# A fused attention and feed-forward stack on one core: half of q's transposes moved, a product in one instruction, the PE stream aligned in the last layer, and the output step split off

## The chip, the core and the metric

The kernel runs on one core of one Trainium2 chip, as one launch. The metric is the device time of a run in microseconds (us). Engines: PE (TensorE, matmuls and transposes; PEld is its weight load), DVE (VectorE), ACT (ScalarE), POOL (GpSimd), and SP, whose queue issues nearly all DMAs. PSUM is the accumulator memory that PE writes and DVE and ACT read; POOL works in SBUF.

## The reference, cut to what matters

Inputs are `x` of 8 x 512 x 128 in float32 and the weights. Two blocks follow one another, each as `x = x + layernorm(block(layernorm(x)))`:

```python
x = x + _layernorm(attn(_layernorm(x)))       # Taylor-expanded attention, 16 heads
y = _layernorm(x)
for i in range(6):                            # DEPTH
    y = attn_layer(shift_tokens(y), Wqkv[i], ...) + y      # local attention, window 32
    y = ffn_layer(shift_tokens(y), ...) + y                # layer norm, 128 -> 2x341, gelu, 341 -> 128
x = x + _layernorm(y)
```

`attn_layer` projects to q, k and v (16 heads of 64), scales q and k to unit length, multiplies by rotary tables (`q*cos + rotate_half(q)*sin`, with scales), takes scores over the block's own and the previous 32 keys, a softmax, and a product with v and `Wo`.

## The kernel before, in words

The first block takes the first 532 us and is not touched. After that the work is cut into **units**: one unit is 128 tokens (`j`, 4 per sequence) of one sequence (`b`, 8) in one layer (`l`, 6), 192 in all. Four units in a row make a **group** (one sequence in one layer). The stream between layers is kept transposed, features on partitions, in `state[b]`.

One pass of the main loop, number t, runs different stages of several units. `at(t, lag, step)` calls a step for unit t - lag; with `ends=True` only where that unit is the last of its group. The order of these calls is PE's order (`manual_schedule(engines={PE})`); a scheduler in the build orders the other engines, by priority (program order; `high_priority` goes first) and its own estimate of when operands are ready. PE's order in one pass before the change:

1. `proj` (lag 0, twice: q, then k): 8 matmuls into a PSUM tile `mm`. DVE multiplies the tile by the tables: `turned(0)`, `turned(1)` (L447, halves exchanged), `straight` (L454). ACT squares it (L462, `sq`); POOL adds the products (L470).
2. `by_keys` (lag 2): 8 transposes of the softmax weights `pe` in two `tr` tiles, copied by ACT to `pT` (L588).
3. `out_project` (lag 3): 16 matmuls into `py` of tag `s`; DVE adds `py` to `state` in two halves (L632).
4. `by_features(0)` (lag 1): 4 transposes of q and 4 of k, a `tr` tile each, copied by ACT to `qT` and `kT` (L536).
5. `weigh_values` (lag 2): 128 small matmuls `po` (L598), tag `s`; DVE multiplies by the softmax's inverse sums (L606, `on`).
6. `by_features(4, 0)`: the other 4 transposes of q, one `tr` tile.
7. `values` (lag 0): 4 matmuls into `mm`, copied later by ACT (L502, in `spread`, which also issues the DMAs that make `v2`).
8. `by_features(4, 1)`: the other 4 transposes of k.
9. By group: `feed_norm` (t%4 = 2), `feed_first` (t%4 = 3), `feed_middle` (t%4 = 0: 12 matmuls with gelu on ACT), `feed_last` (t%4 = 1: 6 matmuls, then DVE adds to `state`, L696).
10. `scores` (lag 1): mask matmuls (L551) and 128 small matmuls `sp` (L558), tag `s`; then a maximum on DVE (L566) and 16 exponentials on ACT (L570).
11. `out_by_features` (lag 2): 8 transposes of `on` in two `tr` tiles, copied by ACT to `oT` (L620).

PSUM tags: `tr` has two buffers of one bank, `mm` two of two banks, `s` **one** of two banks. So a `tr` tile waits until ACT has copied the tile two before it, and `po` waits until the two additions of `py` to `state` are done.

In the last layer `feed_last` also makes the result, in the same step: DVE writes `fs` (L696), PE transposes it (4 transposes, a `tr` tile), DVE takes statistics of that tile in PSUM (L115, L117), ACT makes the inverse root (L104, L106), DVE scales out of PSUM (L127, `fo`), POOL adds `xr` (L707), SP sends it out.

ACT changes its function table twice a group: `gelu_only` (L91) before the gelus, tied behind ACT's last copy to `pT`, and `log_and_exp` (L85) behind the last gelu.

PE's instruction stream is padded at two places: `addr_align(FILL)`, FILL = 16, in `feed_hidden`, and once a group at t%4 = 1 `addr_align(128, offset=IN_STEP)`, which puts the next instruction at place 98 of 128. The condition `t <= len(units) - NB * (B - 1)` is t <= 164, so the last such place is t = 161; passes from 165 on have none.

Of the kernel before, what the change touches and what calls it, by code (L numbers as in the profile page):

```python
# [8 lines left out]
F32 = mybir.dt.float32  # L9
BF16 = mybir.dt.bfloat16  # L10
AF = mybir.ActivationFunctionType
ALU = mybir.AluOpType
# [3 lines left out]
P = 128  # L16
DM = 128
H = 16
# [3 lines left out]
NEG = -(2.0**100)  # L22
EPS = 1e-5
FILL = 16
IN_STEP = 98


@with_exitstack
def sandwich_kernel(ctx: ExitStack, tc: tile.TileContext, ins: dict, out: bass.AP):
    nc = tc.nc  # L30
    x_d = ins["L0_attn_hidden_states"]
    B, N, _ = x_d.shape
    NB = N // P
    assert B >= 2
    DEPTH = ins["L0_ffn_Wqkv"].shape[0]
# [42 lines left out]
    def transposed(ps, src, rows, cols):  # L78
        nc.tensor.transpose(ps[:cols, :rows], src, ident[:rows, :rows])  # L79


    tables, exps, divisions, copies, pcopies, maxima = [], [], [], [], [], []

    def log_and_exp(behind):
        ld = nc.scalar.preload_act_table_set("natural_log_exp_and_others")  # L85
# [3 lines left out]

    def gelu_only():  # L90
        ld = nc.scalar.preload_act_table_set("gelu_and_others")  # L91
        issue_behind(ld, pcopies[-1])
        tables.append(ld)

    def issue_behind(later, earlier):
        tc.add_manual_dep(
            later.ins, earlier.ins.name,
            mybir.DependencyInfo(mybir.DependencyClass.NoSync, mybir.DependencyReason.DATA),
            reason="order on an engine",
        )  # L100
# [7 lines left out]
    def layer_norm(pool, dst, src, nb, by_log=False, later=False):  # L108


        st = pool.tile([P, nb, 6], F32, tag="ln_st", name="ln_st")
        mv = pool.tile([P, nb, 2], F32, tag="ln_mv", name="ln_mv")
        rs = pool.tile([P, nb], F32, tag="ln_rs", name="ln_rs")
        for j in range(nb):
            nc.vector.bn_stats(st[:, j, :], src[:, j, :])  # L115
        for j in range(nb):
            nc.vector.bn_aggr(mv[:, j, :], st[:, j, :])  # L117
        if by_log:
            inverse_root(rs, mv[:, :, 1], eps)
        else:  # L120
            nc.vector.tensor_scalar(rs, mv[:, :, 1], EPS, None, ALU.add)
            nc.scalar.activation(rs, rs, AF.Sqrt)
            nc.vector.reciprocal(rs, rs)

        def last(behind=None):
            for j in range(nb):
                t = nc.vector.tensor_scalar(  # L127
                    dst[:, j, :], src[:, j, :], mv[:, j, 0:1], rs[:, j : j + 1], ALU.subtract, ALU.mult
                )
                if behind is not None:  # L130
                    issue_behind(t, behind)

        if later:
            return last
        last()
# [8 lines left out]
    HF = HD // 2  # L144
# [282 lines left out]
    def proj(u, s):  # L427

        L, b, j = u["L"], u["b"], u["j"]
        wqkv, tab = L["wqkv"], L["tab"]  # L430
        lhs = state[b][:, j * P : (j + 1) * P]
        if s == 0:
            u["ss"] = f2.tile([P, 2, H], F32, tag="ss", name="ss")
            u["qk"] = f2.tile([P, 2, H, 2, HF], F32, tag="qk", name="qk")
        ss, qk = u["ss"], u["qk"]

        ps = psum.tile([P, 2, H, HF], F32, tag="mm", name="mm")
        for a in range(2):
            nc.tensor.matmul(  # L439
                ps[:, a].rearrange("p h d -> p (h d)"), lhs, wqkv[:, s, a, :], start=True, stop=True  # L440
            )
        sq = f2.tile([P, H, 2, HF], F32, tag="sq", name="sq")
        t1 = f2.tile([P, 2, H, HF], F32, tag="t1", name="t1")
        t2 = f2.tile([P, 2, H, HF], F32, tag="t2", name="t2")

        def turned(a):
            nc.vector.tensor_tensor(  # L447
                t2[:, a], ps[:, 1 - a],
                tab[:, 2 * s + 1, j, HF * a : HF * (a + 1)].unsqueeze(1).to_broadcast([P, H, HF]),
                ALU.mult,  # L450
            )

        def straight():
            nc.vector.tensor_tensor(  # L454
                t1, ps,
                tab[:, 2 * s, j, :].rearrange("p (a d) -> p a d", a=2).unsqueeze(2)
                .to_broadcast([P, 2, H, HF]),
                ALU.mult,
            )

        def squared(a):
            nc.scalar.activation(sq[:, :, a, :], ps[:, a], AF.Square)  # L462

        turned(0)
        turned(1)
        straight()
        squared(0)
        squared(1)
        u["sq", s] = sq
        nc.gpsimd.tensor_tensor(qk[:, s].rearrange("p h a d -> p a h d"), t1, t2, ALU.add)  # L470
# [109 lines left out]
    def by_keys(u):  # L580
        pe = u["pe"]
        u["pT"] = pT = f1.tile([P, NP, P], F32, tag="pT", name="pT")
        for c in range(0, NP, 4):
            ps = psum.tile([P, 4, P], F32, tag="tr", name="tr")
            for i in range(4):
                transposed(ps[:, i, :], pe[:, c + i].rearrange("p a k -> p (a k)"), P, P)
            with tc.high_priority():
                pcopies.append(nc.scalar.copy(pT[:, c : c + 4, :], ps))  # L588

    def weigh_values(u):  # L590

# [91 lines left out]
    def feed_last(u):  # L683
        L, l, b, gT = u["L"], u["l"], u["b"], u["gT"]
        py = psum.tile([P, N], F32, tag="mm", name="py")
        for c, (c0, cn) in enumerate(CH):
            nc.tensor.matmul(  # L687
                py, L["w2"][:cn, c, :], gT[:cn, c, :], start=(c == 0), stop=(c == NCH - 1)
            )
        last = l == DEPTH - 1  # L690
        if last:
            fs = f1.tile([P, N], F32, tag="xnT", name="fs")
        for a in range(2):
            r = slice(HD * a, HD * (a + 1))
            sl = state[b][r, a : N + a]
            nc.vector.scalar_tensor_tensor(  # L696
                fs[r] if last else sl, py[r], b2_c[r, l : l + 1], sl, ALU.add, ALU.add
            )
        if last:
            ps = psum.tile([P, NB, P], F32, tag="tr", name="tr")  # L700
            for j in range(NB):
                transposed(ps[:, j, :], fs[:, j * P : (j + 1) * P], P, P)
            fo = f1.tile([P, NB, DM], F32, tag="xn", name="fo")
            layer_norm(f2, fo, ps, NB, by_log=True)
            xr = f1.tile([P, NB, DM], F32, tag="xr", name="xr")
            nc.sync.dma_start(xr, x1[b])
            nc.gpsimd.tensor_tensor(fo, fo, xr, ALU.add)  # L707
            nc.sync.dma_start(out[b].rearrange("(n p) d -> p n d", p=P), fo)

    log_and_exp(None)  # L710
    units = []
# [6 lines left out]
    def at(t, lag, step, *args, ends=False):  # L718
        if 0 <= t - lag < len(units) and (not ends or units[t - lag]["j"] == NB - 1):
            step(units[t - lag], *args)  # L720
# [3 lines left out]
    with tc.manual_schedule(engines={mybir.EngineType.PE}):  # L724
        norm_in(0)
        in_by_features(0)
        project_qk(0)
        project_v(0)
        sums_before(0)
        layers[0] = load_layer(0)  # L730
        for k in range(len(steps) + 2):
            slot(k)
        for t in range(len(units) + 7):
            if t < len(units):
                u = units[t]
                if u["l"] not in layers:
                    layers[u["l"]] = load_layer(u["l"])
                u["L"] = layers[u["l"]]


            gelus = 0 <= t - 5 < len(units) and units[t - 5]["j"] == NB - 1
            at(t, 0, proj, 0)
            at(t, 0, proj, 1)


            if t % NB == 1 and NB < t <= len(units) - NB * (B - 1):
                nc.tensor.addr_align(128, offset=IN_STEP)
            at(t, 2, by_keys)
            if gelus:
                gelu_only()  # L750
            at(t, 3, out_project)

            if t == 0:
                head_norm(NG - 1)
            if t == 1:
                attn_out(B - 1)
            at(t, 1, by_features, 0)
            at(t, 2, weigh_values)
            at(t, 1, by_features, 4, 0)
            at(t, 0, values)  # L760
            if t == 3:
                to_state(B - 1)
            at(t, 0, sum_squares, 0)
            at(t, 0, sum_squares, 1)
            if not gelus:
                at(t, 0, unit_length)
            at(t, 1, by_features, 4, 1)
            at(t, 0, spread)
            at(t, 3, feed_norm, ends=True)
            at(t, 4, feed_first, ends=True)  # L770
            at(t, 5, feed_middle, ends=True)
            if gelus:
                at(t, 0, unit_length)
            at(t, 6, feed_last, ends=True)
            at(t, 1, scores)
            at(t, 3, feed_normed, ends=True)
            at(t, 2, out_by_features)

# [90 lines left out]
```

## Time and profile before

| | us |
|---|---|
| median of 3 runs | 3826.05 (3818.64 to 3838.03) |
| the profiled execution | 3825.62 |
| its span, first to last instruction | 3823.9 |
| first block, up to the first `proj` | 532.3 |
| a group of four units in layers 1 to 4 | 66.5 to 67.0 |
| groups from unit 168 on (last layer) | 69.9, 75.1, 70.0, 74.8, 70.0 |
| from the start of unit 191 to the end | 86.4 |

The profile is of one execution. Its timeline gives the start and length of instructions, merged where neighbours are alike; a difference of two starts is the time that a piece holds the engine. Lengths of PE pieces run over into the next piece, because matmuls are pipelined. The chain of waits names as releaser the instruction that the profile infers; where that had long been done, it was another.

### The profile page before, as it was taken

The page shows a single profiled execution, that of the slowest core. Times are in us where ns is not written, and L with a number is a line of the kernel's source. Part 1 is how long each engine was busy: PE and PEld are TensorE (multiplying, and loading weights), DVE is VectorE, ACT ScalarE, POOL GpSimd, SP SyncE. Part 2 cuts the span into 40 slices and gives each one's busy share as a digit, 9 for nine tenths or more (in the row PEclk, how much of TensorE's full clock was granted, in tenths as well). Part 3 has the DMA queues.
Part 4 walks back from the last instruction along what each step waited for, and adds up shares of the span by engine and source line. Part 5 has one row for each costly group of instructions (what it writes and reads, how often), then busy time and mean ns, then how long its engine had stood idle before and what let it go on. Part 6 is the DMA issues. An engine that isn't in the chain of part 4 may idle for free.

```text
span 3823.9 us, 152697 instructions
## 1 busy us (share of the span) xinstructions
PE 3703.6 (97%) x65600; PEld 2456.2 (64%) x65600; DVE 2794.7 (73%) x4308; ACT 2662.9 (70%) x6750; POOL 1842.6 (48%) x1311
## 2 busy tenths in 40 slices
PE   8999999999999999999999999999999999989997
PEld 4545556666666666666666666666666666666664
DVE  4555567787877778787777778777777878777774
ACT  5565557777777777777777777777777777767665
POOL 0000025555555555555555655555555555555552
PEclk9999999999999999999999999999999999999998
DMA  2000012222232222322222322223222222222221
GB/s 82 17 9 12 6 51 72 60 67 62 73 79 69 66 58 66 81 73 62 67 66 58 88 72 67 57 67 82 71 65 65 67 58 65 65 67 69 64 67 32
DMA packets 153219, 233.66 MB, mean 61 GB/s; under 512 B 32622, under 2 KB 53356, under 8 KB 151788
## 3 DMA queue, kind: packets, MB, share of 16 engines
q1 hardware_dynamic: 152556, 223.89, 22.8%
q8 instruction: 530, 8.68, 0.9%
q14 instruction: 133, 1.09, 0.1%
HBM read 24.54 MB, written 4.19 MB: 8 GB/s over the span
## 4 chain that ended last, share of the span: by engine, by line
PE 95%; issue 2%; ACT 2%; DVE 1%; POOL 0%; DMA 0%; POOLq 0%; SPq 0%; DVEq 0%; ACTq 0%
PE tr L79 20%; PE mm L439 17%; PE py L627 9%; PE mm L497 9%; PE po L598 8%; PE sp L558 8%; PE y L300 4%; PE mm L652 3%; PE mm L654 3%; PE py L687 3%; PE sc L270 3%; PE sp L551 2%; PE vv L248 2%; PE qk L239 1%; PE po L336 1%
## 5 line engine op out<-in xcount | busy, mean ns | idle before, releaser
L470 POOL TENSOR_TENSOR qk<-t,t 128x1024 f32<-128x1024 f32 x384 | 909.9, 2370 | 679.3 <-DVE t L454 405.3
L486 POOL TENSOR_TENSOR qk<-qk,ss 128x1024 f32<-128x1024 f32 x384 | 722.2, 1902 | 16.0
L439 PE MATMUL mm<-wqkv,state 128*128 128x512 f32 x1536 | 698.4, 597 | 2.6 <-ACT v L502 2.6
L447 DVE TENSOR_TENSOR t<-mm,tab 128x512 f32<-128x512 f32 x768 | 498.6, 671 | 239.5 <-PE mm L439 239.5
L570 ACT ACTIVATE pe<-sp,mx 128x64 f32<-128x64 f32 x3072 | 652.1, 381 | 2.3 <-DVE mx L566 2.3
L462 ACT ACTIVATE sq<-mm 128x512 f32<-128x512 f32 x768 | 421.3, 607 | 118.6 <-DVE t L454 114.0
L454 DVE TENSOR_TENSOR t<-mm,tab 128x1024 f32<-128x1024 f32 x384 | 468.4, 1220 | 5.9
L439 PEld LDWEIGHTS mm<-wqkv,state 128*128 128x128 f32 x1536 | 273.7, 191 | 289.6 <-issue 242.2
L473 DVE TENSOR_REDUCE ss<-sq 128x16 f32<-128x1024 f32 x384 | 448.6, 1209 | 0.7 <-ACT sq L462 0.6
L79 PE MATMUL tr<-ident,qk 128*128 128x128 f32 x3072 | 440.7, 276 | 1.8 <-ACT qT L536 0.8
L536 ACT COPY kT<-tr 128x512 f32<-128x512 f32 x384 | 225.6, 587 | 299.6 <-PE tr L79 299.4
L79 PEld LDWEIGHTS tr<-ident,qk 128*128 128x128 f32 x3072 | 351.0, 141 | 120.7 <-issue 100.8
L627 PE MATMUL py<-oT,wo 128*128 128x128 f32 x3072 | 377.4, 276 | 0.5 <-ACT oT L620 0.5
L627 PEld LDWEIGHTS py<-oT,wo 128*128 128x128 f32 x3072 | 364.5, 194 | 0.7 <-ACT oT L620 0.7
L497 PE MATMUL mm<-wqkv,state 128*128 128x512 f32 x768 | 363.1, 595 | 0.3 <-ACT sq L462 0.3
L620 ACT COPY oT<-tr 128x512 f32<-128x512 f32 x384 | 206.8, 589 | 221.5 <-PE tr L79 218.9
L598 PE MATMUL po<-v,pT 64*32 64x64 f32 x24576 | 301.9, 225 | 56.0 <-PE tr L79 49.1
L598 PEld LDWEIGHTS po<-v,pT 64*32 64x32 f32 x24576 | 274.2, 105 | 98.0 <-PE tr L79 88.5
L566 DVE TENSOR_REDUCE mx<-sp 128x16 f32<-128x1024 f32 x192 | 235.1, 1225 | 104.2 <-PE sp L558 104.2
L558 PE MATMUL sp<-kT,qT 64*32 64x64 f32 x24576 | 304.7, 226 | 6.4 <-issue 6.4
L558 PEld LDWEIGHTS sp<-kT,qT 64*32 64x32 f32 x24576 | 270.6, 105 | 62.5 <-issue 60.0
L606 DVE TENSOR_TENSOR on<-po,su 128x1024 f32<-128x1024 f32 x192 | 235.2, 1225 | 96.8 <-PE po L598 96.8
(114 smaller groups left out, 5082.8 us busy)
## 6 DMA issues: line engine op xcount, KB each, us to landing
v<-v SPq DMA_DIRECT2D x1152, 128.0 KB
v<-v SPq DMA_DIRECT2D x672, 64.0 KB
wqkv<-in_L_ffn_Wqkv_dram SPq DMA_DIRECT2D x6, 1536.0 KB
wo<-in_L_ffn_Wo_dram SPq DMA_DIRECT2D x6, 512.0 KB
xin<-_attn_hidden_states_dram SPq DMA_DIRECT2D x8, 256.0 KB
xr<-_attn_hidden_states_dram SPq DMA_DIRECT2D x8, 256.0 KB
x<-xr SPq DMA_DIRECT2D x8, 256.0 KB
xr<-x SPq DMA_DIRECT2D x8, 256.0 KB
```

What stands on the lines that cost most here:

```text
L79: nc.tensor.transpose(ps[:cols, :rows], src, ident[:rows, :rows])
L439: nc.tensor.matmul(ps[:, a].rearrange("p h d -> p (h d)"), lhs, wqkv[:, s, a, :], start=True, stop=True)
L447: nc.vector.tensor_tensor(t2[:, a], ps[:, 1 - a], tab[:, 2 * s + 1, j, HF * a : HF * (a + 1)].unsqueeze(1).to_broadcast([P, H, HF]), ALU.mult,
L454: nc.vector.tensor_tensor(t1, ps, tab[:, 2 * s, j, :].rearrange("p (a d) -> p a d", a=2).unsqueeze(2) .to_broadcast([P, 2, H, HF]), ALU.mult,)
L470: nc.gpsimd.tensor_tensor(qk[:, s].rearrange("p h a d -> p a h d"), t1, t2, ALU.add)
L473: su = nc.vector.tensor_reduce(u["ss"][:, s], u["sq", s].rearrange("p h a d -> p h (a d)"), AX.X, ALU.add)
L486: nc.gpsimd.tensor_tensor(t, t, ss[:, i, :].unsqueeze(2).to_broadcast([P, H, HD]), ALU.mult)
L497: nc.tensor.matmul(ps[:, p, :], lhs, L["wqkv"][:, 2, p, :], start=True, stop=True)
L558: nc.tensor.matmul(sp[W * w : W * (w + 1), p, pair, :], qT[HD * p : HD * (p + 1), pair, W * w : W * (w + 1)], kT[HD * p : HD * (p + 1), pa ...
L570: ex = nc.scalar.activation(pe[:, pair, p, :], sp[:, p, pair, :], AF.Exp, bias=mx[:, p, pair : pair + 1])
L598: nc.tensor.matmul(po[W * w : W * (w + 1), p, pair, :], pT[r, pair, W * w : W * (w + 1)], v2[r, w, HD * pair : HD * (pair + 1)], start=Tru ...
L627: nc.tensor.matmul(py, L["wo"][:, c, :], oT[:, c, :], start=(c == 0), stop=(c == NP - 1))
```

## The change

Five edits:

- `by_features(4, 0)` moves from behind `weigh_values` to ahead of it, directly behind `by_features(0)`.
- `turned` is one DVE instruction of 1024 elements per row with the halves of PSUM read in reverse order (`ps[:, ::-1]`) in place of two of 512.
- `gelu_only` moves behind `by_features(4, 0)` and is tied behind ACT's last copy to `qT` or `kT` and the last exponential (of any inverse root or softmax) in place of the last copy to `pT`.
- IN_STEP is 92 in place of 98, and the alignment goes on to the end (t < 192): seven more places.
- The result of the last layer leaves `feed_last`. A new step `feed_out` follows `scores` in the same pass; for all sequences but the last, ACT copies the transposed tile from PSUM to SBUF first, and the layer norm works on that copy.

```diff
-IN_STEP = 98
+IN_STEP = 92
...
     def gelu_only():
         ld = nc.scalar.preload_act_table_set("gelu_and_others")
-        issue_behind(ld, pcopies[-1])
+        issue_behind(ld, copies[-1])
+        issue_behind(ld, exps[-1])
         tables.append(ld)
...
-        def turned(a):
+        def turned():
             nc.vector.tensor_tensor(
-                t2[:, a], ps[:, 1 - a],
-                tab[:, 2 * s + 1, j, HF * a : HF * (a + 1)].unsqueeze(1).to_broadcast([P, H, HF]),
+                t2, ps[:, ::-1],
+                tab[:, 2 * s + 1, j, :].rearrange("p (a d) -> p a d", a=2).unsqueeze(2)
+                .to_broadcast([P, 2, H, HF]),
                 ALU.mult,
             )
...
-        turned(0)
-        turned(1)
+        turned()
...
-        if last:
-            ps = psum.tile([P, NB, P], F32, tag="tr", name="tr")
-            for j in range(NB):
-                transposed(ps[:, j, :], fs[:, j * P : (j + 1) * P], P, P)
-            fo = f1.tile([P, NB, DM], F32, tag="xn", name="fo")
-            layer_norm(f2, fo, ps, NB, by_log=True)
-            xr = f1.tile([P, NB, DM], F32, tag="xr", name="xr")
-            nc.sync.dma_start(xr, x1[b])
-            nc.gpsimd.tensor_tensor(fo, fo, xr, ALU.add)
-            nc.sync.dma_start(out[b].rearrange("(n p) d -> p n d", p=P), fo)
+    def feed_out(u):
+        b, fs = u["b"], u["fs"]
+        src = ps = psum.tile([P, NB, P], F32, tag="tr", name="tr")
+        for j in range(NB):
+            transposed(ps[:, j, :], fs[:, j * P : (j + 1) * P], P, P)
+        fo = f1.tile([P, NB, DM], F32, tag="xn", name="fo")
+        if b < B - 1:
+            nc.scalar.copy(fo, ps)
+            src = fo
+        layer_norm(f2, fo, src, NB, by_log=True)
+        xr = f1.tile([P, NB, DM], F32, tag="xr", name="xr")
+        nc.sync.dma_start(xr, x1[b])
+        nc.gpsimd.tensor_tensor(fo, fo, xr, ALU.add)
+        nc.sync.dma_start(out[b].rearrange("(n p) d -> p n d", p=P), fo)
...
-            if t % NB == 1 and NB < t <= len(units) - NB * (B - 1):
+            if t % NB == 1 and NB < t < len(units):
                 nc.tensor.addr_align(128, offset=IN_STEP)
             at(t, 2, by_keys)
-            if gelus:
-                gelu_only()
             at(t, 3, out_project)
...
             at(t, 1, by_features, 0)
+            at(t, 1, by_features, 4, 0)
+            if gelus:
+                gelu_only()
             at(t, 2, weigh_values)
-            at(t, 1, by_features, 4, 0)
             at(t, 0, values)
...
             at(t, 1, scores)
+            if t >= 6 + NB * B * (DEPTH - 1):
+                at(t, 6, feed_out, ends=True)
             at(t, 3, feed_normed, ends=True)
             at(t, 2, out_by_features)
```

More of the change, by code (lines that the diff above doesn't have):

```diff
@@ L79, in transposed @@
         nc.tensor.transpose(ps[:cols, :rows], src, ident[:rows, :rows])
-    tables, exps, divisions, copies, pcopies, maxima = [], [], [], [], [], []
+    tables, exps, divisions, copies, maxima = [], [], [], [], []
     def log_and_exp(behind):
@@ L587, in by_keys @@
             with tc.high_priority():
-                pcopies.append(nc.scalar.copy(pT[:, c : c + 4, :], ps))
+                nc.scalar.copy(pT[:, c : c + 4, :], ps)
     def weigh_values(u):
@@ L691, in feed_last @@
         if last:
-            fs = f1.tile([P, N], F32, tag="xnT", name="fs")
+            u["fs"] = fs = f1.tile([P, N], F32, tag="xnT", name="fs")
         for a in range(2):
```

## The prediction

> **What bounds the kernel now.** I read the page first: which engine is full, and whether the chain that ended last runs through it.
>
> ```profile
> PE 3703.6 (97%) x65600; PEld 2456.2 (64%) x65600; DVE 2794.7 (73%) x4308; ACT 2662.9 (70%) x6750; POOL 1842.6 (48%) x1311
> q8 instruction: 530, 8.68, 0.9%
> PE 95%; issue 2%; ACT 2%; DVE 1%; POOL 0%; DMA 0%; POOLq 0%; SPq 0%; DVEq 0%; ACTq 0%
> ```
>
> PE is the bound: the end moves only where PE waits less or gets less to do. The edits remove no PE work, so I look for PE's gaps, by group of four units (busy time by stretch): one of layer 4, two of the last layer.
>
> ```profile
> 2719.00:2785.70 66.70, 65.68 (x1299) 45.09 (x1298) 51.74 (x75) 48.84 (x131) 37.45 (x27) 1.00 0.28 71
> 3319.30:3389.16 69.86, 66.31 (x1304) 45.27 (x1303) 54.40 (x87) 49.42 (x134) 38.80 (x28) 1.00 0.27 68
> 3389.16:3464.29 75.13, 68.28 (x1304) 46.28 (x1303) 54.49 (x87) 49.61 (x134) 38.80 (x28) 0.98 0.25 64
> ```
>
> The last layer's groups are 3.2 and 8.4 us longer. Then the timeline: PE, DVE and ACT in a normal unit (134; it starts at 2756.39).
>
> ```profile
> 2762.51 1.04 PE L79 MATMUL tr<-ident,qk 128*128 128x128 f32 x8
> 2763.82 1.48 PE L598 MATMUL po<-v,pT 64*32 64x64 f32 x128 [0.28 <-PE tr L79]
> 2765.23 0.66 PE L79 MATMUL tr<-ident,qk 128*128 128x128 f32 x4
> 2765.72 1.88 PE L497 MATMUL mm<-wqkv,state 128*128 128x512 f32 x4
> ...
> 2763.14 0.58 DVE L632 TENSOR_TENSOR state<-py,state 64x128 f32<-64x128 f32 x2
> 2763.76 1.22 DVE L454 TENSOR_TENSOR t<-mm,tab 128x1024 f32<-128x1024 f32 x1
> ...
> 2763.14 0.58 ACT L536 COPY qT<-tr 128x512 f32<-128x512 f32 x1 [0.62 <-PE tr L79]
> 2763.63 0.59 ACT L536 COPY kT<-tr 128x512 f32<-128x512 f32 x1
> ```
>
> The 8 transposes start at 2762.51 and take 8 x 0.11 = 0.87 us, to 2763.38; `po` starts 0.44 later. The profile names the transposes as releaser, but they were done; what ends just before is DVE's additions of `py` to `state` (2763.72), which free the one buffer of tag `s`. This is the only gap of a normal unit. Last, PE in unit 173 of the last layer:
>
> ```profile
> 3416.54 1.45 PE L598 MATMUL po<-v,pT 64*32 64x64 f32 x112 [0.28 <-PE tr L79]
> 3420.03 0.35 PE L598 MATMUL po<-v,pT 64*32 64x64 f32 x16 [2.04 <-issue]
> ...
> 3422.95 2.74 PE L687 MATMUL py<-gT,w 128*128 128x512 f32 x6
> 3427.40 0.63 PE L79 MATMUL tr<-ident,fs 128*128 128x128 f32 x4 [1.70 <-DVE fs L696]
> ...
> 3428.39 1.09 PE L558 MATMUL sp<-kT,qT 64*32 64x64 f32 x87
> 3431.53 0.66 PE L558 MATMUL sp<-kT,qT 64*32 64x64 f32 x41 [2.06 <-issue]
> ```
>
> Two kinds of stall: `fs` for 1.70 us, and two of 2.0 us inside a run of like matmuls, with nothing to wait for ("issue"). `po` and `sp` are 128 matmuls with 128 weight loads, 256 instructions in 1.4 us. The page has 530 instruction packets, 8.68 MB, 16.4 KB each; over PE's 131,200 matmuls and loads that is one packet per 248, so every such run crosses into a new packet. I read the 2.0 us stalls as code that had not come. They come in every second group from 173 on (173, 181, 189), where no alignment places the stream any more. Waits of PE from 3319 on: `fs` 13.4 us (8 times), `po` on issue 6.1 (3), `sp` on issue 5.6 (3).
>
> **Part by part.** The sum is made against the profiled execution: 3825.6 us, 1.7 outside its span of 3823.9, and 0.4 below the median.
>
> *The result step.* Six units (169 to 189 in fours) should take 17.28 us, as in layer 4. They take 20.53, 24.07 (with 1.58 more in the next unit, 16.27 for 14.69), 20.73, 25.38, 20.54 and 23.68: 32.8 us too much. Three carry the issue stalls (8.4 + 8.1 + 6.4 = 22.9), three don't (3.25 + 3.45 + 3.26 = 10.0). In one without: 1.86 us from `fs` (L687 holds PE 4.44 for 2.58), 0.47 for 4 transposes, 1.0 because the second half of `out_by_features` waits for a `tr` tile that the layer norm still reads. After: behind `scores`, which take 2.1 us, `fs` is long there: wait 0. The 4 transposes stay: 0.46. The added wait: the third `tr` tile waits for the new copy to `fo`, a copy like `oT`'s, 0.59 us; it ends about 0.7 us after its transposes, and 0.44 of that is covered by the first half of `out_by_features`: 0.35 with the handover. Queued behind it on PE: 4 transposes and the next `proj`; on ACT: two copies and the exponentials, which wait for the maximum anyway. The layer norm (0.9 + 0.4 + 1.4 us on DVE, 0.5 on ACT) is on no chain of PE's, POOL's addition (1.27) fits its gaps; `fo` must have left, about 2.6 us of DMA later, before the next `xn` is written some 12 us on; if it hasn't, DVE waits, and `proj` next. SP's queue carries the send ahead of `v2` transfers wanted a unit later. I take 0.9 a unit, bounds 0.5 to 1.5, so 6 x 0.9 = 5.4 stay.
>
> *In step in the last layer.* If the stalls go, all 32.8 - 5.4 = 27 us are gained; if they stay, 22.9 - 10.0 = 13 us less: 14. Layers 1 to 4 are aligned with the same code between alignments and hold no such stall (46 groups of 66.5 to 67.0), so I take 27. The Trainium skill ("Runtime: NRT & Kernel Launch", section "Instruction fetch mechanics") says that crossing a 16 KiB boundary of the instruction stream is mostly hidden. That speaks against this edit; by it the stalls would have another cause and stay, and the total below would be 13 us worse. The 2.04 and 2.06 us above are such crossings, not hidden, so I go by the rows.
>
> *IN_STEP 98 to 92.* The 4 moved transposes are 8 instructions, so `po` moves from its place by +8 - 6 = +2, what follows by -6. Price nothing if no run falls badly; the rival below if one does.
>
> *Half of q ahead of `po`.* The moved transposes need the `tr` tile of q's first half: ACT's copy ends at 2763.72, the very time at which DVE's additions ended. So the gap stays where it was, ahead of 4 transposes now: start 2763.79 (0.07 after the copy, as `po` was after DVE), 0.44 to 2764.23, `po` 1.41, 0.05 for the change of shape: `values` at 2765.69, before 2765.72. Queued behind this added wait: `po`, `values`, all of the unit. In three of four units `po` takes 1.51 to 1.55 in place of 1.41, its first matmuls 55 and 71 ns apart after the wait. If the transposes cover that start, these units gain 0.07 to 0.14: 0.37 a group; if not, they lose up to 0.1 a group. 46 groups: -17 to +5; I take -8. Cover elsewhere: `on` on DVE comes 0.4 later, in slack (DVE ends its sums at 2768.8, and the next maximum starts at 2770.3); ACT's second copy of q falls in its 0.79 us idle ahead of L462.
>
> *One `turned`.* The two take 1.21 us from start to next start, a `straight` of the same 1024 elements 1.13: 0.08 x 384 = 31 us of DVE, which has gaps. Reverse order isn't in the trace; were it 0.1 dearer, still nothing on PE, unless it moves the additions to `state` (below). 0.
>
> *`gelu_only`.* The load (L91, 1.28 us) stood ahead of q's first copy in gelu units (2793.41 in place of 2792.7); left there it would now hold PE 0.7 us. Behind the copy it pushes L462 by about 1.1, into slack of 1.9 before the gelu product needs that `mm` tile. 0. At the very end ACT now holds gelu's table while it needs logarithms: six loads of 1.28 between 3790 and 3800; tied behind the last exponential, most go, and the `xn` that waits for the sent `fo` comes about 2 us sooner: -2, bounds 0 and -4.
>
> Sum: 3825.6 - 27 - 8 - 2 = 3788.6, say **3788 us**, 1.0% faster. Best ends: -29 (0.5 a unit), -17 and -4, with some 15 us more if DVE's slack shortens waits that I can't see, 3760. Worst ends of the same case: 14, +5 and 0, 3817.
>
> **Rivals.** (a) *Only half of the last layer's loss returns*: the stalls stay, or ACT runs the new copy behind the 16 exponentials (3.3 us a unit, 6 units, -20 of the gain). 3825.6 - 14 - 2 = 3810 without gain elsewhere. For it: ACT's order is the scheduler's, not written. 0.12. (b) *Out of step everywhere, slower*: the new place puts the end of `po` or `sp` on a packet's edge behind the wait for q's copy, so that the next packet is asked for too late. Unit 173 shows the price: 75.13 - 69.86 = 5.3 us in one group of two; 23 pairs of groups give 122, 3788 + 122 = 3910. One run alone: 23 x 2.04 = 47, 3835. It decides from the point at which the code for a `po` is first asked for less than about 2 us before its last matmuls. For it: eight instructions moved, and the margin before was small (ten places less was enough for 173). Against: 92 moves `po` by only 2 places. 0.09. (c) *State added late*: with one `turned`, DVE's scheduler puts `straight` ahead of the additions to `state`; they end 1.2 us later, 2764.95, and `po` waits 0.7 beyond 2764.23: 184 x 0.7 = 129, 3917. Decides once the additions end past 2764.23. Against: they have high priority, and `py` is done at 2762.7. 0.05. (d) *The changes do nothing*: the excess of the last layer has another cause; 3826. 0.02.
>
> **How the numbers follow.** Measurement can tell about 0.5%, 19 us: faster means under 3807, slower over 3845. The forecast has 0.72, nearly all under 3807; (a) 0.12, a third of it under 3807; (b) 0.09, a third of it near 3835; (c) 0.05; (d) 0.02. Faster 0.75, same 0.13, slower 0.12. The range leaves out (b) with two runs and (c) above and some 0.05 below: 3755 to 3828.
>
> **What would show it.** Right: groups from unit 168 at 67 to 68.5 us; no PE wait on issue inside `po` or `sp`; no PE wait on `fs` but at the end; q's 12 transposes with a gap of 0.4 us ahead of the last four, and `po` directly behind them; layers 1 to 4 at 66.3 to 66.8 a group; one L91 and no pairs of table loads at the end. Wrong: `po` still behind a gap, and L632 behind L454 on DVE (c); 2 us gaps in `po` or `sp` in layers 1 to 4 (b); the new copy behind L570 on ACT (a).

## The result, and the profile after

The changed kernel takes 3861.33 us (median of 4 runs, 3860.7 to 3870.13) beside 3826.73 before: a ratio of 1.0093, 95% interval 1.0067 to 1.0120. It is 0.9% **slower**; 1.0% faster was forecast. Its profiled span is 3858.9 us, 35.0 more than before. Lines of L84 and beyond have moved by one or more (L598 is L599, L536 is L537, and so on).

The page's busy times of the changed kernel:

```profile
PE 3729.1 (97%) x65600; PEld 2443.5 (63%) x65600; DVE 2799.7 (73%) x3924; ACT 2668.4 (69%) x6752; POOL 1841.3 (48%) x1311
```

PE still bounds it, with the same number of instructions. The page counts 25.5 us more as busy (3729.1 for 3703.6) and 9.5 more as idle; since the recorded length of a PE piece runs over into what follows, the loss is read below from the starts of the units. The longest waits of PE (engine, line, releaser: us in total, times, longest):

```profile
PE tr L79 <- ACT qT L537: 45.3, 190, 0.2
PE po L599 <- issue: 32.7, 18, 2.2
```

Before, the same tiles had these waits:

```profile
PE po L598 <- PE tr L79: 49.1, 189, 0.6
PE po L598 <- issue: 6.1, 3, 2.0
PE tr L79 <- ACT qT L536: 0.8, 1, 0.8
```

The wait of a normal unit is nearly as long in total as it was, but it stands for ACT's copy of q now. The wait of `po` on issue is new at this size; it is what rival (b) named. By group (busy time by stretch), two neighbours in layer 3 and two of the last layer:

```profile
2424.69:2491.79 67.10, 66.15 (x1301) 44.69 (x1300) 51.90 (x67) 49.12 (x132) 37.55 (x27) 1.00 0.25 63
2491.79:2560.72 68.93, 66.31 (x1300) 45.00 (x1299) 51.88 (x67) 49.07 (x132) 37.53 (x27) 1.00 0.24 62
3377.59:3446.67 69.08, 67.08 (x1305) 45.13 (x1303) 54.95 (x79) 49.95 (x135) 38.77 (x28) 1.00 0.27 69
3446.67:3515.73 69.06, 67.08 (x1305) 45.23 (x1303) 54.95 (x79) 49.95 (x135) 38.75 (x28) 1.00 0.27 69
```

The last layer's alternation of 70 and 75 us is gone, as forecast (69.1 each). In its place about one group of two up to unit 167 is 2 us longer (in three cases 4), and all are some 0.3 longer. From the starts of the units in both traces the 35.0 us add up: +1.0 ahead of unit 0, +1.6 in units 0 to 7, **+55.7 in units 8 to 167**, -19.8 in units 168 to 190, -3.5 from unit 191 on. Of the 55.7, 43.2 lie in every eighth unit (13, 21, 29, ...). The timeline of PE in one of these (unit 117, start 2511.69):

```profile
2517.81 1.04 PE L79 MATMUL tr<-ident,qk 128*128 128x128 f32 x8
2519.09 0.66 PE L79 MATMUL tr<-ident,qk 128*128 128x128 f32 x4 [0.24 <-ACT qT L537]
2519.67 1.30 PE L599 MATMUL po<-v,pT 64*32 64x64 f32 x107
2522.64 0.42 PE L599 MATMUL po<-v,pT 64*32 64x64 f32 x21 [1.66 <-issue]
```

`po` breaks off after 107 of 128 matmuls, always at that one, in 18 of these 20 units; units 13 and 157 have no gap. In three of the 18 (units 61, 101 and 133) the clock that the profile shows as granted to PE falls to half right behind the gap, for 3.4 us: the 0.50 in this row of unit 61 is its share of full speed.

```profile
1566.60:1569.90 3.30, 3.30 (x20) 1.40 (x5) 3.06 (x3) 0.00 (x0) 0.00 (x0) 0.50 0.19 45
```

These three units lose 4 us instead of 2. And a normal unit (134, start 2804.98): PE, DVE, ACT.

```profile
2811.10 1.04 PE L79 MATMUL tr<-ident,qk 128*128 128x128 f32 x8
2812.38 0.66 PE L79 MATMUL tr<-ident,qk 128*128 128x128 f32 x4 [0.24 <-ACT qT L537]
2812.97 1.48 PE L599 MATMUL po<-v,pT 64*32 64x64 f32 x128
2814.38 1.98 PE L498 MATMUL mm<-wqkv,state 128*128 128x512 f32 x4
...
2811.50 0.58 DVE L633 TENSOR_TENSOR state<-py,state 64x128 f32<-64x128 f32 x2
2812.11 0.26 DVE L578 RECIPROCAL su<-su 128x16 f32<-128x16 f32 x1
...
2811.74 0.58 ACT L537 COPY qT<-tr 128x512 f32<-128x512 f32 x1 [0.62 <-PE tr L79]
```

PE's gap is where it was, ahead of the moved transposes, and ends with ACT's copy (2812.32). DVE's additions to `state` now end at 2812.08, 7.10 us into the unit; before it was 7.33 (2763.72 in a unit that starts at 2756.39). They are earlier, and in a normal unit PE no longer waits for them.

### The profile page after: what moved, and what is told of

Its sections match the earlier page's. It is cut to its first block, busy times and chain, and to the rows that moved or that the text cites. A ratio compares the mean times of both kernels' runs of the same rounds, so it can differ in the third digit from the quotient of the medians.

```text
span 3858.9 us, 152309 instructions
## 1 busy us (share of the span) xinstructions
PE 3729.1 (97%) x65600; PEld 2443.5 (63%) x65600; DVE 2799.7 (73%) x3924; ACT 2668.4 (69%) x6752; POOL 1841.3 (48%) x1311
## 4 chain that ended last, share of the span: by engine, by line
PE 90%; ACT 4%; DVE 3%; issue 1%; POOL 0%; DMA 0%; SPq 0%; POOLq 0%; DVEq 0%
PE tr L79 17%; PE mm L440 17%; PE mm L498 9%; PE py L628 9%; PE sp L559 7%; PE po L599 7%; PE y L301 4%; PE mm L653 3%; PE mm L655 3%; PE py L688 3%; ACT qT L537 3%; PE sc L271 3%; PE sp L552 2%; PE vv L249 2%; PE po L337 1%
## 5 line engine op out<-in xcount | busy, mean ns | idle before, releaser
L440 PE MATMUL mm<-wqkv,state 128*128 128x512 f32 x1536 | 697.7, 596 | 5.5 <-DVE xn L128 2.9
L448 DVE TENSOR_TENSOR t<-mm,tab 128x1024 f32<-128x1024 f32 x384 | 468.6, 1220 | 234.8 <-PE mm L440 234.7
L537 ACT COPY kT<-tr 128x512 f32<-128x512 f32 x384 | 225.2, 586 | 377.1 <-PE tr L79 376.8
L456 DVE TENSOR_TENSOR t<-mm,tab 128x1024 f32<-128x1024 f32 x384 | 468.5, 1220 | 7.1 <-POOL qk L471 1.4
L498 PE MATMUL mm<-wqkv,state 128*128 128x512 f32 x768 | 385.6, 625 | 0.2 <-ACT sq L464 0.2
L537 ACT COPY qT<-tr 128x512 f32<-128x512 f32 x384 | 224.9, 586 | 168.8 <-PE tr L79 168.8
L599 PE MATMUL po<-v,pT 64*32 64x64 f32 x24576 | 289.4, 226 | 35.3 <-issue 32.7
L599 PEld LDWEIGHTS po<-v,pT 64*32 64x32 f32 x24576 | 255.4, 105 | 71.0 <-issue 66.8
```

The lines of the kernel that those rows point to most:

```text
L440: nc.tensor.matmul(ps[:, a].rearrange("p h d -> p (h d)"), lhs, wqkv[:, s, a, :], start=True, stop=True)
L448: nc.vector.tensor_tensor(t2, ps[:, ::-1], tab[:, 2 * s + 1, j, :].rearrange("p (a d) -> p a d", a=2).unsqueeze(2) .to_broadcast([P, 2, H, ...
L456: nc.vector.tensor_tensor(t1, ps, tab[:, 2 * s, j, :].rearrange("p (a d) -> p a d", a=2).unsqueeze(2) .to_broadcast([P, 2, H, HF]), ALU.mult,)
L498: nc.tensor.matmul(ps[:, p, :], lhs, L["wqkv"][:, 2, p, :], start=True, stop=True)
L537: copies.append(nc.scalar.copy(dst, ps))
L599: nc.tensor.matmul(po[W * w : W * (w + 1), p, pair, :], pT[r, pair, W * w : W * (w + 1)], v2[r, w, HD * pair : HD * (pair + 1)], start=Tru ...
```

## The experiments

Ratios below are to the kernel before on the same chip, with 95% intervals.

**1 to 4: the place of the stream, and the order.** I read the break in `po` as the edge of an instruction packet. In unit 173 before, the breaks in `po` and in `sp` (prediction) lie 254 matmuls and loads apart, and waits are instructions, too, so I count 256 to a packet. 107 matmuls are 214 instructions, so the edge before lies 256 - 214 = 42 instructions ahead of `po`, give or take one, among `out_project`'s matmuls. PE's program then has three waits for ACT: ahead of q's transposes and of k's (for the copies to `pT`), and ahead of the moved ones (for q's copy). Theory E: what counts is how far ahead of the first of these waits the edge lies. The first three expectations below carry my first count of that distance (12 at IN_STEP = 92 and 24 at 104 in the new order, 15 at 92 and 21 at 98 in the old one); counted with the program's list of waits it is 15 and 27, and 16 and 22.

Only the place:

```diff
-IN_STEP = 92
+IN_STEP = 104
```

> The changed kernel with IN_STEP = 104 in place of 92, nothing else. Theory E (the packet's edge): the 2 us gaps in po, in one unit of eight, come because the edge between two packets of PE's code falls only some 12 instructions ahead of the wait for the first copy of softmax weights (tr of q), so the next packet is asked for after the later wait for q's copy. 104 moves the edge 12 instructions further ahead (24). Then no gap in po, 18 x 2.3 = 41 us less: about 3820 us, and groups of 67.1 throughout. Rival O (the order itself): the moved transposes make po run dry at any place of the edge; the gaps stay, 3861 us.

Measured: 3816.5 us, ratio 0.997 (0.9961 to 0.9979). No gap in `po`; the span is 40.1 us shorter than that of the changed kernel; units 8 to 167 alone are 44.4 shorter. Its waits of PE begin:

```profile
PE tr L79 <- ACT qT L537: 45.5, 190, 0.2
PE tr L79 <- DVE xl L128: 7.7, 1, 7.7
```

The line of `po` on issue is gone, and the wait for q's copy stays. Rival O falls: at this place of the edge the new order has no gaps.

The order undone at that place:

```diff
             at(t, 1, by_features, 0)
-            at(t, 1, by_features, 4, 0)
-            if gelus:
-                gelu_only()
             at(t, 2, weigh_values)
+            at(t, 1, by_features, 4, 0)
+            if gelus:
+                gelu_only()
```

> The changed kernel with half of q's transposes (and the table load tied to them) back behind the weighted values, and IN_STEP = 104, so that the edge stays well ahead of the waits; the single turned product, the later output step and the alignment in the last layer are kept. If the order costs what the traces show apart from the gaps (units 0.03, 0.03, 0.15 and 0.11 us longer: about 13 us in 160), this is 13 us faster than IN_STEP = 104 alone: about 3804 us, with groups of 66.7 in layers 1 to 4 and under 68.5 in the last. Rival: the single turned product or the later output step costs something in every unit; then groups stay at 67.0 and the time at about 3818.

Measured: 3758.31 us, ratio 0.9809 (0.9790 to 0.9828). Faster than I expected by 46 us, and than both kernels: 1.9% below the kernel before. Its unit 134 (start 2724.93):

```profile
2731.05 1.04 PE L79 MATMUL tr<-ident,qk 128*128 128x128 f32 x8
2732.14 1.47 PE L599 MATMUL po<-v,pT 64*32 64x64 f32 x128
...
2731.45 0.58 DVE L633 TENSOR_TENSOR state<-py,state 64x128 f32<-64x128 f32 x2
```

From the first transpose to `po` it is 1.09 us, where the kernel before had 1.31. `po` again starts 0.1 us after DVE's additions, and these end earlier. My expectation left that out; experiments 5 to 7 test it.

The old kernel with the new place:

```diff
-IN_STEP = 98
+IN_STEP = 92
```

> The kernel before with IN_STEP = 92 in place of 98, nothing else: the edge comes 6 instructions later in the stream, about 15 ahead of the wait for the first copy of softmax weights, where 21 had no gaps and 11 or 12 had them. Theory E: gaps of 2 us in po of one unit in eight if 15 is too few (about 3866 us), none if it is enough (3826); the gaps that unit 173 and its like have stay, since the last layer isn't aligned. Rival O: no gaps in layers 0 to 4, since the order is the old one, 3826 us.

Measured: 3884.72 us, ratio 1.0155 (1.0124 to 1.0186). Nothing else is changed, and `po` breaks off in nearly every eighth unit, after 110 matmuls:

```profile
PE po L598 <- issue: 50.3, 23, 2.6
PE po L598 <- PE tr L79: 49.1, 189, 0.6
```

With the first experiment this shows the place 92 as the cause of the gaps in either order; 16 instructions ahead are too few. It is 19 us slower than I expected: in 12 of the 18 eighth units with a gap from 13 to 157 the granted clock falls to half behind it, and these 12 take 22.9 us more together than if they had lost what the other six lose (2.5 us each).

The order alone:

```diff
+            at(t, 1, by_features, 4, 0)
+            if gelus:
+                gelu_only()
             at(t, 2, weigh_values)
-            at(t, 1, by_features, 4, 0)
```

(with the new tie of the table load, and its old call removed)

> The kernel before with half of q's transposes ahead of the weighted values and the table load behind them, IN_STEP = 98, two turned products, the output step as it was. Theory E: the edge keeps its 21 instructions ahead of the wait, so layers 0 to 4 have no 2 us gaps, and the order's own price shows alone: groups of 67.0 in place of 66.7, about 13 us, 3839 us in all. Rival O: gaps of 2 us in po of one unit in eight, about 3875 us. My prediction's sum for this edit was -8 us, 3818.

Measured: 3843.94 us, ratio 1.0035 (1.0020 to 1.0050): slower by 13 us, as theory E says, without gaps in `po` in layers 0 to 4 (the last layer, not aligned here, has four). Its groups there are 67.1 in place of 66.7.

**5 to 7: order and turned product, two by two.** Theory M: the two edits mask each other. One operation ends DVE's additions earlier, which pays only where `po` waits for them; in the new order PE waits for ACT's copy.

```diff
-        turned()
+        turned(0)
+        turned(1)
```

On the kernel with IN_STEP = 104, new order:

> The changed kernel with IN_STEP = 104 and the turned product back in two operations. In the new order q's 12 transposes wait for ACT's copy of the first four, not for DVE. Theory M (the two edits mask each other): the earlier additions to state that one operation brings (end 7.10 in place of 7.34 us into a unit) are worth nothing here, so the time is that of IN_STEP = 104 alone, 3816.5, within 5 us. Rival: the single operation is what costs in the changed kernel (a read of PSUM in reverse); then two operations are faster by 10 us or more.

Measured: 3818.86 us, ratio 0.9969 (0.9957 to 0.9981), beside 0.9970 with one operation. Worth nothing there.

On the kernel with IN_STEP = 104, old order:

> The kernel with half of q's transposes back behind the weighted values and IN_STEP = 104 (3758.3 us), with the turned product back in two operations. Theory M: in this order the weighted values wait for DVE's additions to state, so the gap ahead of them goes from 0.21 back to 0.44 us in each unit: 184 x 0.23 = 42 us slower, about 3800. Rival: the gain of 45 us beyond what I expected of undoing the order comes from elsewhere (the place of the table load, the alignment); then it stays at 3758.

Measured: 3798.58 us, ratio 0.9922 (0.9900 to 0.9944), beside 0.9809. Worth 43 us there. The longest wait of PE in the new order with two operations:

```profile
PE tr L79 <- ACT qT L537: 46.2, 191, 0.8
```

and in the old order with two:

```profile
PE po L599 <- PE tr L79: 46.3, 177, 0.6
```

With two operations the two waits are equal in total, one for ACT and one (filed under the transposes) for DVE. One operation shortens only the second.

On the kernel before, alone (the edit of the change, nothing else):

> The kernel before with the turned product in one operation, nothing else. Theory M: 0.23 us in each of 184 units, 42 us faster, about 3784; the gaps of 2 us in the last layer stay. My prediction's price for this edit was 0: 3826.

Measured: 3787.83 us, ratio 0.9893 (0.9869 to 0.9917), 41 us faster. Theory M stands; units 8 to 167 are 33.4 us shorter in the trace, and the wait of `po` filed under the transposes has gone from 49.1 us to this:

```profile
PE po L598 <- PE tr L79: 0.8, 2, 0.4
```

| at IN_STEP = 104, with the later output step | two `turned` | one `turned` |
|---|---|---|
| half of q behind the weighted values | 0.9922 | **0.9809** |
| half of q ahead of them | 0.9969 | 0.9970 |

**8: in step, alone.**

```diff
-IN_STEP = 98
+IN_STEP = 104
...
-            if t % NB == 1 and NB < t <= len(units) - NB * (B - 1):
+            if t % NB == 1 and NB < t < len(units):
```

> The kernel before with IN_STEP = 104 and the alignment up to the end, nothing else. Theory E: the edge lies 28 instructions ahead of the wait in all layers, so units 173, 181 and 189 lose their gaps (12.5 us of waits on issue, 13 with what follows) and keep the 3.3 us of the output step: 3813 us, groups of 70 in the last layer. Rival: those gaps belong to the output step (its transposes between the last feed-forward matmuls and the scores), and stay: 3826.

Measured: 3811.94 us, ratio 0.9949 (0.9929 to 0.9968). The waits of PE from unit 168 to the last group:

```profile
PE tr L79 <- DVE fs L696: 10.2, 6, 1.7
PE po L598 <- PE tr L79: 6.3, 24, 0.3
PE tr L79 <- DVE fo L127: 4.8, 6, 0.8
```

No wait on issue in `po` or `sp`; six units of 20.53 us, which is the 3.25 of the output step over 17.28. The gaps of units 173, 181 and 189 were the place of the edge.

**9 and 10: how far ahead is enough.** The changed kernel with 95 and with 98, a single run of each.

> The changed kernel with IN_STEP = 95: the edge some 18 instructions ahead of the wait for the first copy of softmax weights (92: 15, 104: 27). Looked at in layers 1 to 4 alone, where only this place differs. Theory E has its limit between 16 (gaps in nearly every eighth unit) and 21 or 22 (none): here gaps in some of the 20 units, and the packet asked for at about 6.2 or 8.5 us into those units; or, if 18 is enough, none and all asked for before 5 us. Rival: the place relative to po counts (42 instructions for 92, 45 here), and gaps stay in 18 of 20.

Measured: gaps in 18 of the 20 eighth units from 13 to 165, all but 13 and 157, as with 92; 3872.67 us. Units 173, 181 and 189 have gaps here as well, which they haven't with 92:

```profile
PE po L599 <- issue: 38.0, 21, 2.2
```

> The changed kernel with IN_STEP = 98, the place of the kernel before: the edge 21 instructions ahead of the wait. Theory E: no gap of 2 us in po in layers 1 to 4, the packet asked for at about 4.7 us into the unit, groups of 67.1. Rival: with the new order 98 is as bad as 92, and the gaps stay.

Measured: no gap in them; 3820.98 us. Its longest wait of PE:

```profile
PE tr L79 <- ACT qT L537: 45.4, 190, 0.2
```

So in the new order 15 and 18 instructions ahead are too few and 21 enough; in the old one 12 and 16 were too few and 22 enough. Too few means gaps in most units, not in all: with 92 there is none in units 13, 157, 173, 181 and 189. The distance to `po` doesn't separate the cases: 42 in the changed kernel (gaps), 42 in the kernel before (none), 45 at 95 (gaps). That the place decides is shown. That it is the distance to the first *wait* is argued: in all these kernels that wait stands behind the same code, so its place and the place of the edge in `out_project` move together.

## Why the prediction was wrong, point by point

**IN_STEP, the step that failed.** I priced it at nothing "if no run falls badly", from where `po` comes to lie (+2). But the alignment moves the edge against the *waits* as well, and these had not moved with `po`: the distance fell from 22 to 15. The evidence was in the lines I quoted: ten places less had been enough for unit 173, and I took 92 as safe because `po` moved by two. Price by the runs: ratio 1.0093 to 0.9970, 47 us; by the traces the 18 units with a gap take 42.0 us more than with 104, 6 of them for the three falls of the clock. Rival (b) had the mechanism, with a chance of 0.09. That its price for one run is 47, too, is partly luck: it counted 23 gaps of 2.04.

**Half of q ahead of `po`: -8 forecast, +18 measured** (0.9922 to 0.9969 with two `turned`). Right: the gap stayed, 1.28 us from the first transpose to the ninth, set by ACT's copy; and the moved transposes do cover the slow start of `po` (1.41 us in all units). Mis-sized: the change of shape, 0.05 in my sum. From the ninth transpose to `po` it takes 0.59 for 0.44, and `values` directly behind `po` 1.82 for 1.72: 0.25, and so 0.20 more a unit, 37 us over 184 units. With the -17 of my sum for the covered start that makes +20. Alone on the kernel before, the order costs 13 us (experiment 4).

**One `turned`: 0 forecast, 0 measured, in part by luck.** I counted 31 us of DVE "which has gaps" and did not follow what stands behind it on DVE: the additions to `state`, the one thing PE waited for. In the trace they end 0.23 earlier, partly because the reciprocal (0.25) now runs behind them. In the new order that is worth nothing; in the old one it is 43 us. I had named DVE's additions as the releaser of the only gap and still priced a DVE edit at nothing: that omission hid the better half of the change. Rival (c) is refuted by the same lines.

**The result step.** Of 32.8 us I expected 5.4 to stay, 0.9 a unit. Unit 169 takes 18.23 for 17.36: 0.87, right. But 170 takes 0.36 more than a normal one and 171 0.63: the layer norm is not clear of PE. In unit 170 (start 3415.89) DVE does its scaling ahead of the additions:

```profile
3421.28 1.56 DVE L128 TENSOR_SCALAR fo<-fo,ln_mv,ln_rs 128x128 f32<-128x128 f32 x1
...
3423.60 0.58 DVE L633 TENSOR_TENSOR state<-py,state 64x128 f32<-64x128 f32 x2
...
3424.23 1.48 PE L599 MATMUL po<-v,pT 64*32 64x64 f32 x128 [0.32 <-DVE state L633]
```

About 1.9 a group stay in place of 0.9. With the stalls away, this step and the tail are worth 0.9949 to 0.9922, about 10 us, where 14 and 2 were forecast; the two intervals overlap, and in the traces units 168 to 190 are 7.0 shorter.

**In step in the last layer.** Forecast 13, measured by itself 0.9949, 19 us (12 to 27), and 12.7 in the trace of units 168 to 190: right. So is the choice of the row over the Trainium skill's sentence ("Runtime: NRT & Kernel Launch", section "Instruction fetch mechanics") that a crossing is mostly hidden: most are (18 such gaps in `po` beside 530 packets in the changed kernel), but at IN_STEP = 92 the others cost 47 us. That the last layer is free of gaps at 92 is luck: at 95, three instructions further from the wait, units 173, 181 and 189 have them. The sum counted 46 groups of layers 1 to 4 as evidence; these layers have 32.

**`gelu_only` and the tail.** From unit 191 on 82.95 us for 86.45, 3.5 less; 2 forecast (0 to 4). A gain isn't shown, though: in the other traces this stretch takes 83.2 to 85.9 us with the later output step (six kernels) and 83.4 to 86.3 without it (four). The pairs of table loads are gone (five loads stood between 3789.97 and 3800, not six): one of 1.28 us stands behind the inverse root at 3833.30.

By ratios to before, in the order measured: alignment -19, output step and table load -10, order +18, one `turned` 0, 92 for 104 +47. That adds up to 36 us, beside 35 measured; each term is good to some 6 to 11 us.

## What to carry to other kernels

Follow a freed microsecond of a side engine to the next instruction on that engine that the bound engine waits for: that, not the engine's busy share, says what it is worth. When two edits touch the same gap, find which releaser comes second, since the edit that shortens the first is then worth nothing, and measure them two by two. Where a stream is aligned by hand, an edit must be priced by where the packet's edge falls against the waits ahead of a dense run of small matmuls, and a run at each neighbouring place is cheap.

## What the runs showed of the hardware that I had not expected

The start of the instruction packet in question (queue q8) has distinct times after the start of the eighth unit. In the kernel before it is about 4.7 us, ahead of all three waits (22 instructions); at 104 in the new order about 4.1. In the changed kernel it is 8.5 to 8.9 in the units with a gap, about 1.1 us after the last wait (for q's copy or DVE's additions, 7.4) is over, and 6.1 to 6.3 in those without (13, 157, and 173, 181 and 189 in the last layer). From 8.5 to the rest of `po` it takes about 2.5 us, and `po` takes 1.4. Why an edge 12 to 18 instructions ahead of a wait is mostly not enough to have the packet asked for before it, and 21 is, stays open, and so does why five units at 92 escape: no run separates the number of instructions from the time that they take. A gap of 2 us can cost 4: the granted clock was 0.5 for 3.4 us or more behind 3 of the 18 gaps of the changed kernel, and behind 12 of 18 in units 13 to 157 of the old order with 92. Why so much more often there stays open, too.
